# A cross-attention and quantized feed-forward block: in the last batch the first 512 queries of three head groups run ahead of all second halves, and the softmax division is done in parts of 8 heads

## The chip, the core and the metric

One core of one Trainium2 chip runs the kernel. The time is the device time of one execution in microseconds, the median of three runs before the change: 1045.96 (1043.35 to 1048.77).

The engines named below run side by side, each through its own list of instructions in order: PE (TensorE, matrix products; PEld is its loading of weights), DVE (VectorE), ACT (ScalarE), POOL (GpSimd) and SP (here only a queue that issues DMAs). An instruction that waits holds up everything behind it on its engine.

## What is computed

```python
# x: (4, 1024, 256); mem: (4, 77, 256); 16 heads of 16
def xattn(x, mem, Wq, Wkv, Wout, bout):
    q = x @ Wq
    k, v = split(concat((mem, x), axis=1) @ Wkv, 2)      # 77 + 1024 keys
    dots = einsum('bhid,bhjd->bhij', q, k) * 16 ** -0.5
    dots = where(j > i + 77, -inf, dots)                 # a query sees mem and what is not after it
    out = einsum('bhij,bhjd->bhid', softmax(dots), v)
    return merge_heads(out) @ Wout + bout

def ffn(x, w_fc, b_fc, w_proj, b_proj):                  # hidden 1024
    h = gelu(lowprec_linear(x, w_fc, b_fc))              # inputs and weights rounded to 3 mantissa
    return lowprec_linear(h, w_proj, b_proj)             # bits, one exponent per 32 elements

x = x + xattn(layernorm(x), mem, ...)
x = x + ffn(layernorm(x), ...)
```

## The kernel before

**Groups.** The 16 heads of a batch are four groups of four, so there are 16 groups `kk` in all, `last` = 15; the last batch is groups 12 to 15. Four heads lie on four 32-row strips of the partitions, so that four matmuls with 32 rows can run in the array side by side. The 1024 queries are two halves `ic` of 512, the 1101 keys nine tiles of 128.

**Two passes.** The scores of a group are computed twice. The first pass (`max_matmul`, L518, with `max_reduce`, L542 and L544 on DVE) gives the largest score of each query, negated by way of the keys: row `MXR` of each 32-row strip of `qT` takes the maximum, and the same row of `kT` holds -1, so that the second pass (`score_matmul`, L582) comes out with the maximum taken away. ACT then takes the exponential (`score_exp`, L593), POOL masks the tiles on the diagonal (L598), and `times_v` (L619) multiplies by the values. A column of ones beside the values gives the sum of each query's row.

**Order.** `score_pieces` lists 14 pieces of keys by queries: five for the first 512 queries (widths 512, 461, 333, 205, 77), nine for the second (five of 512, then 461, 333, 205, 77). `max_pieces` has 14 pieces of the same widths. `run(kk, extras)` walks over the 14 pieces, each in two half-steps of two heads: in `half_step` the maxima of group `kk + 1` and the scores of group `kk` alternate on PE. The product with the values follows one piece later (`LAG`, the list `late`). Group 15 has no maxima beside it (`last_step`). After piece 1 and after the first half's maxima `put_max` turns 32x32 blocks on DVE (L552), writes them to DRAM and reads them back into row `MXR` of `qT`, two DMAs on SP, long before they are needed.

**Other work among the half-steps.** Each call of `run` takes a list of units; after every half-step it begins units whose turn has come and whose `ready` holds, and `tick` emits the later stages of those begun. The units are: loading and norm of the next batch, projections to q, k and v, and for the batch before: `divide_unit` (softmax division), `wout_unit` (output projection and residual, L716 to L724), `root_unit` (inverse standard deviation by three Newton steps, on POOL while attention runs, L162 to L168), `in_unit` (norm L220/L224, rounding L183 to L206, turn L775), `hidden_unit` (first linear layer L794 and L799, Gelu L805) and `out_unit` (rounding L183 to L206, turn L846, second layer L854 and L857, residual L861, store). A unit covers 128 tokens, a tile; a batch has eight. `helper[0]` is POOL during attention and DVE at the end; POOL does the second rounding step (L206) always.

**Division.** `pack` copies a finished group (L641), places it in `o_pk` by DMA, and writes its row sums to DRAM (L646). When all four groups of a half are packed, `divide_unit(b, ic)` reads the 16 rows of sums spread over 128 partitions (L664), inverts them (L670), writes them (L672), reads each of the 16 rows back over 16 partitions (L678, 16 issues on SP), and multiplies `o_pk` in two products of 128x512 (L687). `rb` has one buffer.

**The last batch.** Groups 12 to 15 carry the units of batch 2. With group 15 come the output projections of the first half of batch 3, if it is divided in time. After the last product a list (`todo`) holds the rest: division of the second half, and for all eight tiles of batch 3 projection, norm, hidden layer and output, DVE being the helper.

**PSUM.** `ps_st` (two buffers of two banks) holds scores and hidden rows, `ps_s` (three banks) maxima and everything small, `ps_av` (one bank) the product with the values.

Of the kernel before, what the change touches and what calls it, by code (L numbers as in the profile page):

```python
# [13 lines left out]
ALU = mybir.AluOpType  # L14
# [29 lines left out]
def kernel(  # L44
# [185 lines left out]
    with ExitStack() as actx:  # L230
# [6 lines left out]
        rbp = ap("rbp", 1)  # L237
# [324 lines left out]


# [67 lines left out]
        divided = set()  # L631
# [26 lines left out]
        def divide_unit(b, ic):  # L658
            got = {}

            def fetch():
                held["rb"] += 1
                got["sm"] = small.tile([P, ICW // SPH], F32, name="sm", bufs=2)
                nc.sync.dma_start(  # L664
                    out=got["sm"], in_=sums.pop((b, ic)).rearrange("h (s j) -> (h s) j", s=SPH)
                )

            def invert():
                r = small.tile([P, ICW // SPH], F32, name="r", bufs=2)
                nc.vector.reciprocal(r, got["sm"])  # L670
                got["rd"] = dram.tile([HEADS, ICW], F32, name="rd")
                nc.sync.dma_start(out=got["rd"].rearrange("h (s j) -> (h s) j", s=SPH), in_=r)  # L672
                got["rb"] = rbp.tile([P, KC, ICW], F32, name="rb")
# [10 lines left out]
            def scale_sums(k):  # L684
                def emit():
                    o = o_pk[b, ic][:, k, :]
                    helper[0].tensor_tensor(o, o, got["rb"][:, k, :], ALU.mult)  # L687
                    if k == KC - 1:
                        divided.add((b, ic))
                        held["rb"] -= 1  # L690
                return emit

            fetch.ready = lambda: packed.get((b, ic)) == NG and not held["rb"]
            stages = [fetch, (4, invert)]
            stages += [(LATER if h == 0 else 1, spread(h)) for h in range(0, HEADS, 2)]
            return cost(0.6, stages + [(4, scale_sums(0)), (2, scale_sums(1))])
# [7 lines left out]
        def wout_unit(b, it):  # L704
# [25 lines left out]
            fetch.ready = lambda: (b, ic) in divided and len(x2) - done["out"] < X2  # L730
# [241 lines left out]
        def run(kk, extras):  # L972
# [8 lines left out]
            rate = sum(price(u) for u in extras) / (2 * sum(length[:-1]))  # L981
            share = 0.0
            for n in range(STEPS):
                for pair in range(2):
# [12 lines left out]
                    if n == 1 and pair == 0 and kk >= 0:  # L997
                        put_max(kk, 1)
                    if n == HALF_AT + 2 and pair == 0 and kk + 1 < B * NG:
                        put_max(kk + 1, 0)  # L1000
# [31 lines left out]
        for kk in range(last + 1):  # L1032
# [15 lines left out]
            if g == NG - 1:  # L1048
                urgent += [divide_unit(b, 0), divide_unit(b, 1)]
# [24 lines left out]
            if kk == last:  # L1074
                helper[0] = nc.vector
                extras += wout_units(b, 0) + [root_unit(b, 0)]
            run(kk, extras)
        while late:
# [48 lines left out]
```

## Time and profile before

| | us |
|---|---|
| median of three runs | 1045.96 |
| the profiled execution | 1048.25 |
| its span | 1046.5 |
| PE busy | 981.6 |
| DVE busy | 652.6 |
| ACT busy | 564.9 |
| POOL busy | 360.0 |
| group 13 with the maxima of 14 | 803.7 to 866.2 |
| group 14 with the maxima of 15 | 866.2 to 921.8 |
| group 15 alone, to its last product | 921.8 to 964.2 |
| after the last product | 964.2 to 1046.5 |
| largest idle gaps of PE between 30 and 960 | 2.54 (at 801.0), 2.41 (562.5), 2.40 (319.4), 1.01 (384.3) |

A row of PE is busy from its start to a modelled end, and a wait for a buffer hidden in it does not show; the distance between equal instructions does. "PEclk" is the clock that TensorE was granted, 1.00 being full: at 0.50 every matmul takes about twice as long. A row of the timeline gives start, duration, engine, line, operation, tiles and shapes, and in brackets the engine's idle time before it with what ended it. A row of the busy times by stage gives the stretch, its length, for each engine the busy time with the number of instructions, then the clock, the share of the DMA engines and GB/s.

### The profile page before, as it was taken

What the parts mean: (1) busy time and instruction counts of PE and PEld (TensorE: products, weight loads), DVE (VectorE), ACT (ScalarE), POOL (GpSimd) and SP (SyncE); (2) the same over time, 40 slices, a digit from 0 to 9 for tenths busy, and PEclk for the clock granted to TensorE, in tenths of its full rate; (3) what the DMA queues carried; (4) which work ended last, traced back from release to release, by engine and by line L of the source; (5) the groups of instructions that cost most, each with busy time, mean ns of one, the idle gap of its engine ahead of it and who ended that gap; (6) DMA issues with size and microseconds to landing.
All of it is one profiled execution on the core that took longest, in us unless ns stands there. A gap on an engine that the chain in (4) does not pass through costs nothing.

```text
span 1046.5 us, 21087 instructions
## 1 busy us (share of the span) xinstructions
PE 981.6 (94%) x8024; PEld 416.2 (40%) x8024; DVE 652.6 (62%) x2127; ACT 564.9 (54%) x838; POOL 360.0 (34%) x751
## 2 busy tenths in 40 slices
PE   4899999999999999999998999999998999999677
PEld 2343434343433344344444344334443334334233
DVE  3587775666484756566475665746557476652785
ACT  4235664555464655655454665665554565666233
POOL 1012422132234444342434253424335246242233
PEclk9899999999998999999998999999997899989576
DMA  3021000202120001101220001100121000001200
GB/s 105 22 67 50 13 26 8 70 13 80 47 73 8 7 10 46 28 7 38 82 70 23 8 15 34 36 11 20 27 69 41 23 8 23 12 13 50 63 21 21
DMA packets 36172, 36.31 MB, mean 35 GB/s; under 512 B 14067, under 2 KB 29747, under 8 KB 36070
## 3 DMA queue, kind: packets, MB, share of 16 engines
q1 hardware_dynamic: 34958, 33.90, 11.8%
q8 instruction: 63, 1.03, 0.4%
q10 hardware_dynamic: 1112, 1.06, 0.3%
q14 instruction: 39, 0.32, 0.1%
HBM read 16.58 MB, written 5.25 MB: 21 GB/s over the span
## 4 chain that ended last, share of the span: by engine, by line
PE 79%; DVE 9%; ACT 3%; DMA 2%; POOL 2%; issue 2%; SPq 1%; POOLq 0%; ACTq 0%; DVEq 0%
PE s_ps L518 35%; PE av_ps L619 16%; PE s_ps L441 6%; PE st_ps L582 5%; PE s_ps L412 3%; PE st_ps L794 3%; PE s_ps L716 3%; DVE jk L544 3%; PE s_ps L854 2%; PE st_ps L799 2%; ACT pt L593 2%; DVE mx L542 1%; PE s_ps L846 1%; DVE amaxh L183 1%; PE s_ps L373 1%
## 5 line engine op out<-in xcount | busy, mean ns | idle before, releaser
L518 PE MATMUL s_ps<-kT,qT 32*128 32x512 f32 (+2 forms) x1736 | 491.8, 537 | 15.0 <-DVE mxp L544 8.2
L593 ACT ACTIVATE pt<-st_ps 128x1024 f32<-128x1024 f32 (+4 forms) x448 | 353.1, 793 | 271.6 <-PE st_ps L582 245.0
L582 PE MATMUL st_ps<-qT,kT 32*128 32x512 f32 (+5 forms) x1792 | 482.4, 534 | 7.4 <-ACT pt L593 6.9
L518 PEld LDWEIGHTS s_ps<-kT,qT 32*128 32x128 f32 x1736 | 194.5, 187 | 189.8 <-issue 70.5
L598 POOL TENSOR_SCALAR_AFFINE_SELECT pt<-pt 128x254 f32<-128x254 f32 (+3 forms) x320 | 117.4, 370 | 431.9 <-ACT pt L593 428.3
L544 DVE CUSTOM_DVE_ANT_0 jk<-s_ps,tri,mx 128x77 bf16<-128x77 f32 (+3 forms) x372 | 174.2, 505 | 97.9 <-PE st_ps L582 63.6
L619 PE MATMUL av_ps<-pt,vaug 128*32 128x256 f32 (+7 forms) x3072 | 223.8, 365 | 2.4 <-POOL hq L206 1.2
L544 DVE CUSTOM_DVE_ANT_0 jk<-s_ps,tri 128x512 bf16<-128x512 f32 (+3 forms) x248 | 126.7, 549 | 142.8 <-PE st_ps L582 103.0
L542 DVE TENSOR_REDUCE mx<-s_ps 128x1 f32<-128x512 f32 x248 | 159.4, 683 | 85.6 <-PE st_ps L582 70.3
L582 PEld LDWEIGHTS st_ps<-qT,kT 32*128 32x128 f32 (+1 forms) x1792 | 186.5, 184 | 21.2 <-ACT pt L593 17.8
L619 PEld LDWEIGHTS av_ps<-pt,vaug 128*32 128x32 f32 (+1 forms) x3072 | 62.3, 109 | 194.7 <-issue 136.6
L206 POOL TENSOR_TENSOR hq<-h,magh 128x512 bf16<-128x512 f32 x64 | 68.4, 1072 | 34.6 <-DVE h L205 27.7
L205 POOL TENSOR_TENSOR h<-h,magh 128x512 f32<-128x512 f32 x40 | 42.0, 1049 | 51.6 <-DVE magh L194 51.1
L701 ACT COPY y<-s_ps 128x256 f32<-128x256 f32 x64 | 23.9, 374 | 49.7 <-PE s_ps L720 24.4
L805 ACT ACTIVATE h<-st_ps 128x1024 f32<-128x1024 f32 x32 | 32.8, 1024 | 30.0 <-PE st_ps L799 29.9
L794 PE MATMUL st_ps<-wfcT,xqT 128*128 128x512 bf16 x128 | 45.0, 439 | 1.8 <-ACT xqT L778 1.8
L183 DVE TENSOR_REDUCE amaxh<-h 128x16 f32<-128x512 f32 x64 | 42.7, 675 | 5.4 <-ACT h L805 5.4
L716 PE MATMUL s_ps<-wo_sb,o_pk 128*128 128x256 f32 x128 | 42.5, 459 | 1.6 <-DVE o_pk L687 1.6
L544 DVE DVE_READ_ACCUMULATOR2_ANT mxp<- 128x1 f32 x512 | 42.0, 82 | 0.0
L412 PE MATMUL s_ps<-wv,xT 128*128 128x256 f32 (+1 forms) x144 | 40.9, 410 | 1.0 <-DVE mx L542 1.0
L441 PE MATMUL s_ps<-xT,wk_sb 128*128 128x512 f32 (+1 forms) x96 | 39.0, 534 | 0.0
L854 PE MATMUL s_ps<-wprT,hT 128*128 128x256 bf16 x256 | 36.4, 289 | 2.6 <-ACT hT L849 2.6
(105 smaller groups left out, 795.2 us busy)
## 6 DMA issues: line engine op xcount, KB each, us to landing
kT<-k_st SPq DMA_DIRECT2D x16, 275.2 KB
xn<-in_x_dram SPq DMA_DIRECT2D x16, 256.0 KB
qT<-q_st SPq DMA_DIRECT2D x16, 256.0 KB
o_pk<-o_st SPq DMA_DIRECT2D x32, 128.0 KB
rb<-rd SPq DMA_DIRECT2D x128, 32.0 KB
x<-in_x_dram SPq DMA_DIRECT2D x32, 128.0 KB
out_dram<-x SPq DMA_DIRECT2D x32, 128.0 KB
x<-in_L_ffn_w_fc_dram SPq DMA_DIRECT2D x8, 128.0 KB
```

Of the source, the lines that this page charges most:

```text
L206: nc.gpsimd.tensor_tensor(dst.rearrange("p (n k) -> p n k", k=QBLK), src3, magb, ALU.subtract)
L412: nc.tensor.matmul(vp[:nj, :], xT[b][:, k, jt * P : jt * P + nj], wv[:, k, :], start=(k == 0), stop=(k == KC - 1),)
L441: nc.tensor.matmul(pp[:, :n], w[:, k, hi * P : (hi + 1) * P], xT[b][:, k, first + lo : first + lo + n], start=(k == 0), stop=(k == KC - 1),)
L518: nc.tensor.matmul(sp[:, 0 : hi - lo], qTs[kk % NQK][rows, it * P : (it + 1) * P], kTs[kk % NQK][rows, lo:hi], start=True, stop=True,)
L542: nc.vector.tensor_reduce(into, sp[:, 0:w], axis=AX.X, op=ALU.max)
L544: nc.vector.tensor_tensor_reduce(junk.tile([P, ICW], BF16, name="jk")[:, 0:w], sp[:, 0:w], mask, 1.0, before, ALU.add, ALU.max, into)
L582: nc.tensor.matmul(st[:nj, e, : i1 - i0], kTs[kk % NQK][rows, t * P : t * P + nj], qTs[kk % NQK][rows, i0:i1], start=True, stop=True,)
L593: nc.scalar.activation(pt[:nj, :, :w], st[:nj, :, :w], AF.Exp, scale=scale)
L598: nc.gpsimd.affine_select(out=pt[:nj, :, :behind], in_=pt[:nj, :, :behind], compare_op=ALU.is_ge, fill=0.0, base=base, pattern=[[0, 2], [1 ...
L619: nc.tensor.matmul(acc[c * PAD : (c + 1) * PAD, off + lo : off + hi], vaugs[b % 2][:nj, t, v0 : v0 + PAD], pts[kk, n, c // 2][:nj, c % 2, ...
L716: nc.tensor.matmul(yp, o_pk[b, ic][:, k, it * P % ICW : it * P % ICW + P], wo_sb[:, k, :], start=(k == 0), stop=False,)
L794: nc.tensor.matmul(hp[:, n, :], xqT[t][:, k, :], wfcT[:, k, n * ICW : (n + 1) * ICW], start=(k == 0), stop=False,)
```

## The change

Three things. First, `divide_unit(b, ic, k)` now divides the 8 heads of part `k`; for all batches it is queued after groups 1 and 3, with four `rb` issues per stage, and `rb` has two buffers of half the size. Second, the groups 13, 14 and 15 run in the order: first halves of 13, 14, 15, then second halves of 13, 14, 15; the maxima of the next group run beside them as before, by halves. Third, where a half's maxima are needed by the stage that follows at once (groups 14 and 15, each half), `next_max` first finishes the products that are outstanding and `add_max` then copies the maxima into a cleared tile (128x512, in the space of the other batch's values), lets TensorE transpose it in four 128x128 blocks into a PSUM tile, and adds this to the half of `qT` on DVE; the DMAs of `put_max` are left out there. Among the second halves stand the units of the first half of batch 3 (projection, norm, hidden layer, output); the list after the last product holds those of the second half alone.

```diff
-        rbp = ap("rbp", 1)
+        rbp = ap("rbp", 2)
...
+        def add_max(kk, half):
+            NI = ICW // P
+            wide = vaugs[(B - 2) % 2].rearrange("p j n -> p (j n)")[:, 0:ICW]
+            nc.vector.tensor_copy(
+                wide.rearrange("p (i c r) -> p c i r", i=NI, r=PAD)[:, :, :, MXR],
+                mxps[kk % 2][:, half * HPG * NI : (half + 1) * HPG * NI].rearrange(
+                    "p (c i) -> p c i", i=NI
+                ),
+            )
+            tp = s_tile([P, ICW])
+            for i in range(NI):
+                nc.tensor.transpose(
+                    tp[:, i * P : (i + 1) * P], wide[:, i * P : (i + 1) * P], ident
+                )
+            q = qTs[kk % NQK][:, half * ICW : (half + 1) * ICW]
+            nc.vector.tensor_tensor(q, q, tp, ALU.add)
+
+        def clear_wide():
+            nc.gpsimd.memset(vaugs[(B - 2) % 2].rearrange("p j n -> p (j n)")[:, 0:ICW], 0.0)
...
-        def divide_unit(b, ic):
+        def divide_unit(b, ic, k):
             got = {}
+            SPK = P // HPC
             def fetch():
                 held["rb"] += 1
-                got["sm"] = small.tile([P, ICW // SPH], F32, name="sm", bufs=2)
+                got["sm"] = small.tile([P, ICW // SPK], F32, name="sm", bufs=2)
...
             def spread(h):
                 def emit():
-                    for i in range(h, h + 2):
+                    for i in range(h, h + 4):
                         nc.sync.dma_start(
-                            out=got["rb"][i % HPC * HD : (i % HPC + 1) * HD, i // HPC, :],
+                            out=got["rb"][i * HD : (i + 1) * HD, :],
                             in_=got["rd"][i, :].partition_broadcast(HD),
                         )
                 return emit
...
+            def scale_sums():
+                o = o_pk[b, ic][:, k, :]
+                helper[0].tensor_tensor(o, o, got["rb"], ALU.mult)
+                divided[b, ic] = k + 1
+                held["rb"] -= 1
+            fetch.ready = lambda: packed.get((b, ic), 0) >= (k + 1) * HPC // HPG and held["rb"] < 2
+            return cost(0.6, [fetch, (4, invert), (2, spread(0)), (1, spread(4)), (3, scale_sums)])
...
-        for kk in range(last + 1):
+        for kk in range(last - 2):
...
-            if g == NG - 1:
-                urgent += [divide_unit(b, 0), divide_unit(b, 1)]
+            if g % 2:
+                urgent += [divide_unit(b, ic, g // 2) for ic in range(NIC)]
...
+            if g == 0 and b == B - 1:
+                extras.append(clear_wide)
             run(kk, extras)
+        b, f = B - 1, B - 2
+        urgent += [divide_unit(b, ic, k) for k, ic in ((0, 0), (1, 0), (0, 1), (1, 1))]
+        early, late_steps = range(HALF_AT + 1), range(HALF_AT + 1, STEPS)
+        def next_max(kk, half, unit=None):
+            if unit is not None and unit[0].ready():
+                begin(unit.pop())
+            while late:
+                k2, n2 = late.popleft()
+                times_v(k2, n2, 0)
+                times_v(k2, n2, 1)
+            tick()
+            add_max(kk, half)
+        outs = [out_unit(t) for t in T]
+        ins = [in_unit(t) for t in T]
+        burst = [hidden_unit(T[:HN])]
+        run(last - 2, [root_unit(f, 1)], early)
+        next_max(last - 1, 0, burst)
+        run(last - 1, burst + outs[:2] + ins[HN : HN + 2], early, False)
+        next_max(last, 0)
+        run(last, ins[HN + 2 :] + outs[2:3], early, False)
+        out2 = outs[3:HN] + [hidden_unit(T[HN:])] + outs[HN : HN + 1]
+        run(last - 2, out2 + wout_units(b, 0), late_steps, False)
+        next_max(last - 1, 1)
+        T = range(b * NT, b * NT + HN)
+        ins = [in_unit(t) for t in T]
+        run(last - 1, outs[HN + 1 :] + [root_unit(b, 0)] + ins, late_steps, False)
+        next_max(last, 1)
+        helper[0] = nc.vector
+        run(last, [hidden_unit(T)] + [out_unit(t) for t in T], late_steps, False)
...
-        T = range((B - 1) * NT, B * NT)
-        todo = urgent + carry
-        chain = lambda ts: [f for t in ts for f in (in_unit(t), hidden_unit([t]), out_unit(t))]
-        todo += merge(chain(T[:HN]), wout_units(B - 1, 1)) + [root_unit(B - 1, 1)]
-        todo += chain(T[HN:])
+        T = range(b * NT + HN, (b + 1) * NT)
+        todo = urgent + wout_units(b, 1) + [root_unit(b, 1)] + carry
+        todo += [f for t in T for f in (in_unit(t), hidden_unit([t]), out_unit(t))]
```

`run` takes the range of pieces as `steps`, and leaves `put_max` out with `puts=False`.

More of the change, by code (lines that the diff above doesn't have):

```diff
@@ L630 @@
         packed = {}
-        divided = set()
+        divided = {}
         def pack(b, ic, g, acc):
@@ L656 @@
         SPH = P // HEADS
-        def divide_unit(b, ic):
+        def divide_unit(b, ic, k):
             got = {}
+            SPK = P // HPC
             def fetch():
                 held["rb"] += 1
-                got["sm"] = small.tile([P, ICW // SPH], F32, name="sm", bufs=2)
+                got["sm"] = small.tile([P, ICW // SPK], F32, name="sm", bufs=2)
                 nc.sync.dma_start(
-                    out=got["sm"], in_=sums.pop((b, ic)).rearrange("h (s j) -> (h s) j", s=SPH)
+                    out=got["sm"],
+                    in_=sums[b, ic][k * HPC : (k + 1) * HPC, :].rearrange("h (s j) -> (h s) j", s=SPK),
                 )
             def invert():
-                r = small.tile([P, ICW // SPH], F32, name="r", bufs=2)
+                r = small.tile([P, ICW // SPK], F32, name="r", bufs=2)
                 nc.vector.reciprocal(r, got["sm"])
-                got["rd"] = dram.tile([HEADS, ICW], F32, name="rd")
-                nc.sync.dma_start(out=got["rd"].rearrange("h (s j) -> (h s) j", s=SPH), in_=r)
-                got["rb"] = rbp.tile([P, KC, ICW], F32, name="rb")
+                got["rd"] = dram.tile([HPC, ICW], F32, name="rd")
+                nc.sync.dma_start(out=got["rd"].rearrange("h (s j) -> (h s) j", s=SPK), in_=r)
+                got["rb"] = rbp.tile([P, ICW], F32, name="rb")
             def spread(h):
                 def emit():
-                    for i in range(h, h + 2):
+                    for i in range(h, h + 4):
                         nc.sync.dma_start(
-                            out=got["rb"][i % HPC * HD : (i % HPC + 1) * HD, i // HPC, :],
+                            out=got["rb"][i * HD : (i + 1) * HD, :],
                             in_=got["rd"][i, :].partition_broadcast(HD),
@@ L682, in spread @@
                 return emit
[L684 to L696, printed above, removed]
+            def scale_sums():
[5 more added lines that the diff above has]
+            return cost(0.6, [fetch, (4, invert), (2, spread(0)), (1, spread(4)), (3, scale_sums)])
         def evacuate(ps):
@@ L728, in collect @@
                 done["wout"] += 1
-            fetch.ready = lambda: (b, ic) in divided and len(x2) - done["out"] < X2
+            fetch.ready = lambda: divided.get((b, ic)) == KC and len(x2) - done["out"] < X2
             return cost(1.8, [fetch, project, (2, add), (2, collect)])
@@ L970, in last_step, with run @@
                 score_exp(kk, n, pair, sts[pair])
-        def run(kk, extras):
+        def run(kk, extras, steps=None, puts=True):
             extras = carry + list(extras)
@@ L980, in run @@
             length = [150 + p[3] - p[2] for p in PIECES]
-            rate = sum(price(u) for u in extras) / (2 * sum(length[:-1]))
+            steps = steps or range(STEPS)
+            rate = sum(price(u) for u in extras) / (2 * sum(length[n] for n in steps[:-1]))
             share = 0.0
-            for n in range(STEPS):
+            for n in steps:
                 for pair in range(2):
@@ L996, in run @@
                             late.popleft()
-                    if n == 1 and pair == 0 and kk >= 0:
+                    if puts and n == 1 and pair == 0 and kk >= 0:
                         put_max(kk, 1)
-                    if n == HALF_AT + 2 and pair == 0 and kk + 1 < B * NG:
+                    if puts and n == HALF_AT + 2 and pair == 0 and kk + 1 < B * NG:
                         put_max(kk + 1, 0)
@@ L1073 @@
                     extras += side[:1] + qs + merge(vs, side[1:])
-            if kk == last:
-                helper[0] = nc.vector
-                extras += wout_units(b, 0) + [root_unit(b, 0)]
+            if g == 0 and b == B - 1:
+                extras.append(clear_wide)
             run(kk, extras)
+        b, f = B - 1, B - 2
[27 more added lines that the diff above has]
+        run(last, [hidden_unit(T)] + [out_unit(t) for t in T], late_steps, False)
         while late:
```

## The prediction

> **What bounds the kernel now.** I read the page first (span, and the row of the granted clock), then the busy time by stage from group 13 to the end, TensorE's idle gaps in its timeline, and the end of the chain of waits.
>
> ```profile
> span 1046.5 us, 21087 instructions
> ...
> PEclk9899999999998999999998999999997899989576
> ```
>
> The clock of TensorE is full but for short dips a batch apart and the last three slices. "Early" below means the five pieces of a group for the first 512 queries, "late" the nine for the second.
>
> ```profile
> core 0: us, PE busy (x) PEld busy (x) DVE busy (x) ACT busy (x) POOL busy (x), PEclk, DMA share, GB/s
> 803.70:866.16 62.46, 61.88 (x498) 24.96 (x494) 37.40 (x124) 34.64 (x47) 23.98 (x46) 0.89 0.05 13
> 866.16:921.78 55.62, 54.59 (x495) 21.86 (x491) 35.73 (x117) 35.47 (x50) 24.67 (x50) 1.00 0.05 17
> ...
> 964.17:1012.23 48.06, 33.66 (x140) 15.41 (x140) 36.62 (x107) 15.77 (x26) 11.86 (x12) 0.72 0.16 47
> 1012.23:1046.50 34.27, 24.43 (x100) 9.33 (x100) 21.81 (x50) 10.65 (x16) 11.45 (x12) 0.60 0.06 20
> ```
>
> Groups 13 and 14 are TensorE's. Group 15 takes 42.4 us, 921.8 to 964.2. What follows its last product, 82.3 us, is a chain of latencies: TensorE is idle 24 us of it and has a clock of 0.72 and 0.60 in the rest. The change works on these 82 us, and on a gap a batch apart, of which this is the last:
>
> ```profile
> 796.53 1.28 POOL L687 TENSOR_TENSOR o_pk<-o_pk,rb 128x512 f32<-128x512 f32 x1
> ...
> 799.44 1.09 ACT L224 ACTIVATE xh<-x,shift,rstd 128x256 f32<-128x256 f32 x2 [3.37 <-POOL shift L168]
> ...
> 800.98 0.41 PE L582 MATMUL st_ps<-qT,kT 32*77 32x77 f32 x1 [2.54 <-ACT pt L593]
> ```
>
> GpSimd's division product (L687) delays the last Newton step of the norm; ScalarE, already at the norm, waits; its exponentials wait behind, then TensorE. The clock pays more than the gap:
>
> ```profile
> 800.00:805.00 5.00, 4.02 (x36) 2.42 (x38) 4.69 (x19) 2.79 (x8) 3.45 (x6) 0.56 0.00 0
> ...
> 815.00:820.00 5.00, 5.00 (x39) 2.13 (x37) 2.22 (x9) 2.52 (x4) 0.82 (x2) 0.74 0.18 56
> ...
> 930.00:935.00 5.00, 5.00 (x60) 2.21 (x55) 0.97 (x2) 2.84 (x5) 4.21 (x7) 0.63 0.04 15
> ```
>
> Half clock from about 800.6 to 817.6 costs 8.5 us. The gaps at 317.0 and 560.1 (2.40 and 2.41 us, TensorE behind VectorE) bring half clock for 10.2 us each, 5.1 us lost. Two gaps of 0.69 and 0.82 us within 4 us, at 924 and 927, bring 6.8 us of it (3.4 lost). A lone gap of 0.70 (939.7) brings none. So between 0.7 and about 1.1 us of idleness in some 3.4 us, the clock halves for 6.8 us or more.
>
> **The change part by part.** Changes count against this execution's span; the execution took 1048.25 us in all, 2.3 above the median of 1045.96, and I put the sum on the median.
>
> *The end, after the last product.*
>
> ```profile
> 965.91 1.69 DMA sums<-o_st
> 967.61 1.80 DMA sm<-sums
> 969.44 0.56 DVE r L670
> 970.02 1.59 DMA rd<-r
> ```
>
> From 964.2 to the first issue of `rb` at 971.6 nothing changes (7.4; the reciprocal is half as wide, no credit). Sixteen issues took 7.55 us on SP; eight remain, 3.8. They land 1.8 later (the row above), the product is 0.7 on VectorE: 13.8. Then four projections at half clock, 2.0 + 0.34 each as at 989.5, less one half that now stands before the wait: 8.3. Evacuation, add and statistics of the last 1.4, inverse root 3.4 (1008.9 to 1012.3), and the second half's chain, unchanged in order, 34.3. On SP two stores of the first half's results now stand ahead of `rd`; their adds end 2.1 after the last product (1.2 + 0.4 + 0.4), `rd` is due at 5.9. Sum 61.2 against 82.3: **-21.1**. Below it can go by some 3 us if the projections find full clock (1.27 each).
>
> *The first half's work moves in among the attention.* Per tile at full clock: projection 1.27, turn 0.21, hidden layer 1.63 (910.35 to 916.87 is four), turn of the hidden row 0.55, output 1.19: 4.85. Four tiles 19.4; one output (1.2) stays behind the last product: **+18.2**. This is the point that decides: TensorE pays for nearly all that the end saves. Not all: where maxima run, a half-step is longer than its matmuls.
>
> ```profile
> 891.31 0.64 PE L619 MATMUL av_ps<-pt,vaug 128*32 128x256 f32 x8
> 891.88 1.05 PE L854 MATMUL s_ps<-wprT,hT 128*128 128x256 bf16 x8
> 893.93 0.64 PE L619 MATMUL av_ps<-pt,vaug 128*32 128x256 f32 x8
> 895.82 0.64 PE L619 MATMUL av_ps<-pt,vaug 128*32 128x256 f32 x8
> ```
>
> A bare half-step takes 1.89 (893.93 to 895.82); one with an output of 1.19 takes 2.62, so 0.73 is paid and about 0.4 is hidden behind the wait for VectorE's maxima. In the order of the changed program some nine pieces (three projections, and three turns and three outputs of batch 2 that stood in group 15) come to lie there: **-3.6** (0 to -8).
>
> *Maxima by TensorE.* Four `put_max` go: four 0.2 us VectorE transposes and eight DMAs on SP, both with room, nothing gained. In their place, four times: a VectorE copy 128x16 (0.2 by the 128x32 transpose at L552), four transposes (sixteen at L373 took 3.68: 0.92), a VectorE add 128x512 (0.69 to 1.11 by L687's rows on VectorE). Transposes: **+3.7** (up to 5.2 by L373's mean of 324 ns). The wait: every score of the next stage is queued on TensorE behind the add. Ahead of group 14 one max matmul lies between (and the hidden burst or projections cover copy and drain): 0.5 each, twice. Ahead of group 15's early half nothing does: 0.85, and 0.35 for the output that waits for its copy. Ahead of its late half the products wait for a mask that stands on GpSimd behind two 0.62 us roundings: 1.2 + 0.9. Together **+4.3** (1.5 to 9).
>
> *Ramps.* Each half drains its products and starts without any under the maxima, and in group 15 the hidden burst takes two table loads (1.28) and four Gelus (1.02) from a ScalarE that paces it: **+1.8** (0 to 5).
>
> *Clock.* Group 15's early half has its dip already. Ahead of the late half 2.1 us idle is over the bound, so one more dip of 6.8 us: **+3.5** (0 to 14, if all four stages dip).
>
> The page "TensorE: Matmul & The Clock Gate" (section "Why this matters for your kernels") warns only of idle gaps over about 3 us; by it this term is nothing and the sum 3.5 lower, but the rows here dip after 2.4 us and after 0.69 + 0.82, and they decide. The same page (Part 4) says that transposes do not count as busy in the same way, which speaks against this change: by it each transition idles 0.9 us more, all four dip, and the sum is 10 higher; no row here shows it.
>
> *Division in parts.* Per batch four units for two; 128 issues of `rb` as before, eight more `sm`, `rd` and reciprocals, on SP and VectorE off the path. What matters is where the GpSimd product stands. In the new order none stands in the norm at the start of a batch. At 801 the norm starts 1.2 earlier, the gap shrinks to 1.3, and I take three windows of half clock for five: **-4.6** (-1.2 to -11). At 317 and 560 a VectorE magnitude took 1.04 us under L687 and 0.38 is left under the rounding that follows (0.61): 0.55 each, gap 1.85, clock as before: **-1.1** (0 to -15). The products' new places meet VectorE elsewhere; they cost nothing while VectorE is 60% busy, as at the start of each batch now.
>
> Sum: -21.1 + 18.2 - 3.6 + 3.7 + 4.3 + 1.8 + 3.5 - 4.6 - 1.1 = +1.1, so **1047 us**.
>
> **The rivals.** *The clock falls at each new transition* (slower). Place: before early 14, early 15, late 14, late 15. Price: 3.4 to 5.1 each, three more than I counted, 10 to 15: about 1060. It decides once idleness passes 1.1 us in 3.4; the transposes' neighbours are light products, and 924 to 927 shows that such work dips. Against it: a dense burst or projections stand before two of the four.
>
> *The batch stalls close* (faster). If the shortened gaps fall under the bound at 801 (another -6.4) and one of 317 and 560 (-6.9 with its rest): 1034. For it: 1.3 us is near the bound. Against: the four tiles' magnitudes still stand in one row on VectorE.
>
> *Group 15 swallows the moved work* (faster). Its 42.4 us hold only about 31 us of matmuls (scores 11.7 and products 12.1 by rows of their widths at full clock, 7.0 of batch 2); the rest waits for exponentials and at half clock. If the hidden layers and outputs fill that, -8: 1039. Against: they bring 8 us to ScalarE too.
>
> *The move does not happen*: excluded, since in the new order only one output of the first half follows the last product.
>
> **How the numbers follow.** The forecast (1040 to 1054 its own range) 0.48; clock at the transitions 0.25; batch stalls 0.14; group 15 0.13. A measurement can tell 0.5%, 5.2 us, from no change. Of the forecast 0.34 lies within that, 0.11 above, 0.03 below; of the slower rival 0.01 within; so faster 0.30, same 0.35, slower 0.35. The range 1034 to 1060 reaches to the other cases.
>
> **What would show it.** After the last product some 61 us, with eight `rb` issues; the last product of group 15 some 21 us later than 964 less what the batch stalls give; idle gaps of 0.5 to 2 us before the four stages and the clock row beside each; at 317 and 560 gaps near 1.9, at 800 near 1.3 with a shorter dip. I am wrong if the half clock after the last product lasts less, if the half-steps of 13 and 14 hide more or less than 0.4 us a piece, or if a transition idles over 3 us.

## The result, and the profile after

The changed kernel takes 1076.24 us (median of 4 runs, 1072.08 to 1077.12), against 1047.05 for the kernel before in the same comparison (1043.35 to 1048.77): a ratio of 1.0263, 95% interval 1.0232 to 1.0293. It is slower by 29 us. The prediction was 1047 us, no change, with a range up to 1060: wrong. The profiled execution has a span of 1075.0 us for 1046.5, 28.5 longer, and these are placed below.

The page of the changed kernel, its span and its row of granted clocks (40 slices):

```profile
span 1075.0 us, 21156 instructions
...
PEclk9889999999998989999999999999997889995956
```

The dip a batch apart is still there at 810 (the seven after the long row of nines), now with the two eights of the reordered groups behind it, and there is a new hole, the 5 that is fourth from the end: group 15's late half. By stages, one line each: early halves of groups 13, 14, 15, late halves of 13, 14, 15, what follows the last product (window, its length, busy time of TensorE, weight loads, VectorE, ScalarE, GpSimd, then the granted clock, DMA share, GB/s):

```profile
810.39:842.88 32.49, 32.34 (x223) 13.27 (x219) 13.50 (x58) 16.01 (x25) 11.78 (x25) 0.79 0.05 15
842.88:867.57 24.69, 21.27 (x174) 9.51 (x174) 16.77 (x61) 12.12 (x18) 17.96 (x37) 0.79 0.07 18
867.57:884.04 16.47, 13.20 (x113) 5.38 (x113) 3.69 (x10) 9.00 (x17) 10.82 (x19) 0.79 0.08 26
884.04:927.82 43.78, 43.18 (x381) 18.45 (x377) 25.40 (x67) 27.48 (x35) 17.84 (x27) 1.00 0.11 32
927.82:970.66 42.84, 36.90 (x335) 16.89 (x334) 32.77 (x93) 22.45 (x32) 27.30 (x49) 0.96 0.08 20
970.66:1016.88 46.22, 42.63 (x287) 15.43 (x287) 14.85 (x27) 25.80 (x33) 13.60 (x18) 0.70 0.03 10
1016.88:1075.00 58.12, 32.11 (x129) 13.86 (x129) 29.25 (x79) 14.72 (x24) 11.44 (x12) 0.63 0.10 30
```

Length times one less the clock is what a stage lost to the throttle, if TensorE paces it. With that the two executions compare like this (us; the stages of before are 803.70 to 964.17 and what follows):

| part | before | after | difference |
|---|---|---|---|
| to the start of group 13 | 803.7 | 810.4 | +6.7 |
| groups 13 to 15, without the clock's loss | 150.2 | 175.4 | +25.2 |
| groups 13 to 15, lost to the clock | 10.3 | 31.1 | +20.8 |
| after the last product | 82.3 | 58.1 | -24.2 |
| span | 1046.5 | 1075.0 | +28.5 |

The second and fourth rows are the trade that the change makes, and they nearly cancel, as forecast (+24.4 and -21.1 there). The loss is in the other two. The largest piece is one place, the transition from group 14's late half to group 15's. TensorE's timeline there (start, length, engine, line, operation, tiles, count, and in brackets the idle time before it and what ended it):

```profile
963.73 0.84 PE L642 MATMUL av_ps<-pt,vaug 128*32 128x167 f32 x16
968.00 0.49 PE L642 MATMUL av_ps<-pt,vaug 77*32 77x77 f32 x8 [3.44 <-POOL pt L621]
...
968.82 1.06 PE L577 MATMUL s_ps<-ident,vaug 128*128 128x128 f32 x4
970.66 2.09 PE L605 MATMUL st_ps<-qT,kT 32*128 32x512 f32 x8 [0.78 <-DVE qT L581]
...
973.94 1.01 PE L815 MATMUL st_ps<-wfcT,xqT 128*128 128x512 bf16 x2 [0.65 <-ACT pt L616]
...
985.78 3.40 PE L605 MATMUL st_ps<-qT,kT 32*128 32x512 f32 x8
991.93 3.00 PE L605 MATMUL st_ps<-qT,kT 32*128 32x512 f32 x8 [2.75 <-ACT pt L616]
```

(An fp32 matmul shows as two records, so x8 are four matmuls.) The last product waits 3.44 us for a mask (L621) on GpSimd. GpSimd was not idle; its own timeline shows what stood ahead of the two masks:

```profile
962.84 0.73 POOL L882 TENSOR_TENSOR x<-x,y 128x256 f32<-128x256 f32 x1
963.52 0.62 POOL L205 TENSOR_TENSOR xh<-xh,magx 128x256 f32<-128x256 f32 x1
964.22 0.62 POOL L206 TENSOR_TENSOR xq<-xh,magx 128x256 bf16<-128x256 f32 x1
964.79 0.62 POOL L205 TENSOR_TENSOR xh<-xh,magx 128x256 f32<-128x256 f32 x1
965.49 0.63 POOL L206 TENSOR_TENSOR xq<-xh,magx 128x256 bf16<-128x256 f32 x1
966.08 0.32 POOL L621 TENSOR_SCALAR_AFFINE_SELECT pt<-pt 77x152 f32<-77x152 f32 x1
966.38 0.61 POOL L205 TENSOR_TENSOR xh<-xh,magx 128x256 f32<-128x256 f32 x1
967.06 0.62 POOL L206 TENSOR_TENSOR xq<-xh,magx 128x256 bf16<-128x256 f32 x1
967.63 0.32 POOL L621 TENSOR_SCALAR_AFFINE_SELECT pt<-pt 77x152 f32<-77x152 f32 x1
```

An add and six roundings of the first half's input units. And the clock, in windows of 1 us (the granted clock is the third number from the end):

```profile
967.00:968.00 1.00, 0.00 (x0) 0.00 (x0) 0.00 (x0) 0.00 (x0) 0.94 (x3) 0.65 0.00 0
...
997.00:998.00 1.00, 1.00 (x5) 0.52 (x8) 0.00 (x0) 0.00 (x0) 0.00 (x0) 0.50 0.00 0
998.00:999.00 1.00, 1.00 (x15) 0.29 (x12) 0.00 (x0) 0.27 (x1) 0.00 (x0) 0.99 0.00 0
```

It falls about 2.7 us into the idle time and comes back 30 us later, some 15 us of work lost: the hidden layer of four tiles (L815, L820) takes 11.8 us, to the next scores, for 6.5 at full clock, and a second wait of 2.75 us for ScalarE follows it.

### The profile page after: what moved, and what is told of

It reads as the page before. It is cut to its first block, busy times and chain, and to the rows that moved or that the text cites. A ratio compares the mean times of both kernels' runs of the same rounds, so it can differ in the third digit from the quotient of the medians.

```text
span 1075.0 us, 21156 instructions
## 1 busy us (share of the span) xinstructions
PE 994.9 (93%) x8040; PEld 421.0 (39%) x8040; DVE 639.5 (59%) x2098; ACT 569.7 (53%) x844; POOL 382.5 (36%) x789
## 3 DMA queue, kind: packets, MB, share of 16 engines
q10 hardware_dynamic: 1112, 1.06, 0.3%
## 4 chain that ended last, share of the span: by engine, by line
PE 74%; POOL 7%; DVE 7%; ACT 4%; issue 3%; DMA 3%; SPq 1%; POOLq 0%; ACTq 0%; DVEq 0%
PE s_ps L518 31%; PE av_ps L642 14%; PE s_ps L441 6%; PE st_ps L605 5%; PE s_ps L737 3%; PE s_ps L412 3%; PE st_ps L815 3%; PE s_ps L875 2%; ACT pt L616 2%; DVE mx L542 2%; PE st_ps L820 2%; DVE jk L544 2%; POOL pt L621 2%; POOL h L205 1%; POOL hq L206 1%
## 5 line engine op out<-in xcount | busy, mean ns | idle before, releaser
L518 PE MATMUL s_ps<-kT,qT 32*128 32x512 f32 (+2 forms) x1736 | 497.1, 540 | 15.0 <-DVE mxp L544 6.9
L605 PE MATMUL st_ps<-qT,kT 32*128 32x512 f32 (+5 forms) x1792 | 489.1, 545 | 10.4 <-ACT pt L616 8.5
L621 POOL TENSOR_SCALAR_AFFINE_SELECT pt<-pt 128x254 f32<-128x254 f32 (+3 forms) x320 | 117.9, 372 | 439.3 <-ACT pt L616 436.6
L544 DVE CUSTOM_DVE_ANT_0 jk<-s_ps,tri,mx 128x77 bf16<-128x77 f32 (+4 forms) x372 | 173.7, 505 | 88.9 <-PE st_ps L605 63.7
L605 PEld LDWEIGHTS st_ps<-qT,kT 32*128 32x128 f32 (+1 forms) x1792 | 188.7, 186 | 26.9 <-ACT pt L616 18.9
L642 PEld LDWEIGHTS av_ps<-pt,vaug 128*32 128x32 f32 (+1 forms) x3072 | 62.5, 109 | 195.8 <-issue 138.0
L205 POOL TENSOR_TENSOR h<-h,magh 128x512 f32<-128x512 f32 x48 | 50.3, 1048 | 56.9 <-DVE magh L194 45.3
L815 PE MATMUL st_ps<-wfcT,xqT 128*128 128x512 bf16 x128 | 45.5, 443 | 2.6 <-ACT xqT L799 1.3
L441 PE MATMUL s_ps<-xT,wk_sb 128*128 128x512 f32 (+1 forms) x96 | 39.2, 536 | 0.0
L870 ACT COPY hT<-s_ps 128x1024 bf16<-128x1024 bf16 x32 | 32.3, 1013 | 11.8 <-PE s_ps L867 11.2
```

The costliest lines, as they stand in the source:

```text
L441: nc.tensor.matmul(pp[:, :n], w[:, k, hi * P : (hi + 1) * P], xT[b][:, k, first + lo : first + lo + n], start=(k == 0), stop=(k == KC - 1),)
L518: nc.tensor.matmul(sp[:, 0 : hi - lo], qTs[kk % NQK][rows, it * P : (it + 1) * P], kTs[kk % NQK][rows, lo:hi], start=True, stop=True,)
L544: nc.vector.tensor_tensor_reduce(junk.tile([P, ICW], BF16, name="jk")[:, 0:w], sp[:, 0:w], mask, 1.0, before, ALU.add, ALU.max, into)
L605: nc.tensor.matmul(st[:nj, e, : i1 - i0], kTs[kk % NQK][rows, t * P : t * P + nj], qTs[kk % NQK][rows, i0:i1], start=True, stop=True,)
L621: nc.gpsimd.affine_select(out=pt[:nj, :, :behind], in_=pt[:nj, :, :behind], compare_op=ALU.is_ge, fill=0.0, base=base, pattern=[[0, 2], [1 ...
L642: nc.tensor.matmul(acc[c * PAD : (c + 1) * PAD, off + lo : off + hi], vaugs[b % 2][:nj, t, v0 : v0 + PAD], pts[kk, n, c // 2][:nj, c % 2, ...
```

## The experiments

Ratios are against the kernel before, on the same chip, with 95% intervals. Theories: the clock at the transitions (A); the masks behind GpSimd's roundings, which bring it about (B); the division in parts, through SP's queue (C); and the rival to all three, that the reordered work itself costs more than the end saves (D).

### Each part of the change alone

`parts_only` is the kernel before with the new `divide_unit`, two `rb` buffers and this:

```
-            if g == NG - 1:
-                urgent += [divide_unit(b, 0), divide_unit(b, 1)]
+            if g % 2:
+                urgent += [divide_unit(b, ic, g // 2) for ic in range(NIC)]
```

> The kernel before with the division in parts alone, the order of the last batch untouched. If the parts cost what the trace of after shows up to the start of group 13 (6.7 us later, with new dips of the clock at 387 and 632 us), less the 3.8 us that eight issues of rb fewer save after the last product, it is about 3 us slower than before (0.3%), with the start of group 13 near 810. If those 6.7 us were a chance of that one execution, the batch stalls give what I forecast, 5.7, and the end 3.8: some 9 us faster.

1056.41 us, 1.0107 (1.0053 to 1.0161): slower by about 9, more than C asked. Group 13 starts at 808.9 (803.7 before). Group 0, ahead of any division, ends between 113.2 and 120.3 us in the profiled executions, so it has to be taken out: from its end to the start of group 13 the two executions with the old division take 687.8 us (before) and 686.6 (`order_only`, below), the six with the parts and nothing else changed up to there 692.5 to 695.4. So the parts cost some 5 to 9 us ahead of group 13. The batch stall at 801 does shrink: its gap is 1.28 for 2.54, and group 13 loses 1.2 us to the clock for 6.9. But what follows the last product takes 88.3 us for 82.3, with a clock of 0.60 for 0.67.

`order_only` is the changed kernel with the old, whole division:

```
-        urgent += [divide_unit(b, ic, k) for k, ic in ((0, 0), (1, 0), (0, 1), (1, 1))]
+        urgent += [divide_unit(b, 0), divide_unit(b, 1)]
```

> The changed kernel with the division of before (whole, one rb buffer), the new order of the last batch kept. If the loss lies in the last batch, group 13 starts near 804 as before, the last batch is as slow as in after and the end some 4 us longer for its sixteen issues of rb: 1071 to 1075, still 2.5% slower than before. If the loss came from the parts, it comes down to within 1% of before.

1064.50 us, 1.0178 (1.0131 to 1.0226), so 17 us slower: the two parts of the change add up to nearly its whole loss, and both lose. Its groups 13 to 15 take 192.6 us for 160.5 (10 of the 32 are the clock's) and its end 65.2 for 82.3. The loss is less than expected, and the trace says why. Its late half of group 15:

```profile
959.50:997.00 37.50, 34.02 (x283) 13.39 (x285) 15.91 (x42) 25.80 (x34) 14.64 (x33) 0.95 0.05 16
```

37.5 us at 0.95 for 46.2 at 0.70. The input units wait for the projections, these for the division, and the whole division ends later: so the roundings fell behind the transition by themselves, and TensorE idles 0.78 us there, not 3.44. The loss at that place takes both parts of the change together.

### The transition ahead of group 15's late half

`filled` gives TensorE something to do in the 3.44 us and leaves the wait as it is:

```
+            for _ in range(5):
+                nc.tensor.matmul(sp, ident, kTs[0][:, 0:ICW], start=True, stop=True)
             while late:
```

> The changed kernel with five idle-filling fp32 matmuls 128x512 (about 0.75 us each at full clock) on TensorE ahead of the last four products of group 14's late half, where it now idles 3.44 us; the wait itself stays. If the clock is the cost (it falls at the end of that idle time and stays at half for 30 us), it stays at full now, the late half of group 15 takes about 35 us for 47.5, and the time falls by some 11 to 13 us to about 1064. If the wait and the light work of the last group are the cost, whatever stands before, the time is within 3 us of after.

1070.60 us, 1.0222 (1.0183 to 1.0262): 5.6 us less than the changed kernel, half of what A said. Its TensorE:

```profile
962.61 4.56 PE L1108 MATMUL s_ps<-kT,ident 128*128 128x512 f32 x10
967.10 0.69 PE L642 MATMUL av_ps<-pt,vaug 128*32 128x205 f32 x16
...
969.34 1.14 PE L605 MATMUL st_ps<-qT,kT 32*128 32x512 f32 x8 [0.78 <-DVE qT L581]
...
983.93 3.00 PE L605 MATMUL st_ps<-qT,kT 32*128 32x512 f32 x8 [2.75 <-ACT pt L616]
```

The spare work covers the wait (L1108; five matmuls, 0.9 us each), the next scores take 1.14 us for 2.09 and the clock is full up to 982: idle time was what brought it down. The second wait of 2.75 us, for ScalarE behind the Gelus, now brings a dip of its own. The stage takes 39.2 us; it lost 10.4 us less to the clock and became 7.1 shorter; presumably some of ScalarE's work had been hidden behind the slow TensorE.

`late_ins` takes the cause of the wait away:

```
-        run(last - 1, outs[HN + 1 :] + [root_unit(b, 0)] + ins, late_steps, False)
+        run(last - 1, outs[HN + 1 :] + [root_unit(b, 0)], late_steps, False, 4.8)
...
-        run(last, [hidden_unit(T)] + [out_unit(t) for t in T], late_steps, False)
+        run(last, ins + [hidden_unit(T)] + [out_unit(t) for t in T], late_steps, False)
```

(4.8 keeps the pace of the units that stay.)

> The changed kernel with the four input units of the first half of batch 3 moved from the end of group 14's late half to the start of group 15's, so that no rounding stands ahead of the last masks on GpSimd. If the masks' place behind the roundings makes the 3.44 us, the idle time there falls to 1.0 to 1.5 us; if the clock then stays up, the late half of group 15 comes to 34 to 37 us and the time to about 1062; if the clock dips but the dense fp32 work that now follows brings it back in 7 us, about 1065. If the half clock belongs to the work of group 15's late half, the time falls by 2 to 3 us only.

1066.09 us, 1.0178 (1.0124 to 1.0232), 10 under the changed kernel. Its TensorE at the same place:

```profile
962.61 1.30 PE L642 MATMUL av_ps<-pt,vaug 128*32 128x167 f32 x24
964.30 0.66 PE L577 MATMUL s_ps<-ident,vaug 128*128 128x128 f32 x4 [0.39 <-DVE vaug L569]
965.74 1.14 PE L605 MATMUL st_ps<-qT,kT 32*128 32x512 f32 x8 [0.78 <-DVE qT L581]
968.07 2.05 PE L605 MATMUL st_ps<-qT,kT 32*128 32x512 f32 x8 [1.19 <-ACT pt L616]
971.29 3.00 PE L605 MATMUL st_ps<-qT,kT 32*128 32x512 f32 x8 [1.18 <-ACT pt L616]
```

No product waits for a mask: B holds for the wait. The late half of 14 is 5.0 us shorter, that of 15 7.7. Two waits of 1.2 us for exponentials still make the clock dip (the scores at 971 take 3.00 us), and it is back some 6 us after the work resumed.

`burst_test` asks why the clock stayed down for 30 us in the changed kernel and for 6 here. It adds ten spare fp32 matmuls 128x256 (the identity by a weight) to the changed kernel, in `hidden_unit`:

```
+                if tiles[0] == (B - 1) * NT:
+                    warm(10)
```

> The changed kernel with ten spare fp32 matmuls 128x256 ahead of the hidden layer (bf16) of group 15's late half, where the clock is at half and stays there for 18 us of dense work. If it is this kind of work that doesn't bring the clock back, as fp32 does in 6 to 7 us, the ten (9 us at half clock) bring it to full ahead of or early in the hidden layer, which then takes 6.5 to 8 us for 11.9; the time stays within 5 us of after. If the clock stays down for some other reason for 30 us, the ten only add some 9 us to the time and the hidden layer takes 11.9 again.

1074.43 us (2 runs), 1.0246 (1.0188 to 1.0304). The wait for the mask is the same 3.43 us, and the clock is at half from 966.1. Then, on TensorE:

```profile
972.88 6.23 PE L962 MATMUL s_ps<-wo_sb,ident 128*128 128x256 f32 x20
978.95 0.38 PE L817 MATMUL st_ps<-wfcT,xqT 128*128 128x512 bf16 x1
...
985.69 1.02 PE L605 MATMUL st_ps<-qT,kT 32*128 32x512 f32 x2
```

and the clock, in windows of 2 us:

```profile
974.00:976.00 2.00, 2.00 (x7) 1.55 (x6) 0.00 (x0) 1.98 (x4) 0.00 (x0) 0.50 0.00 0
976.00:978.00 2.00, 2.00 (x10) 1.77 (x9) 0.00 (x0) 0.44 (x1) 0.00 (x0) 0.92 0.00 0
```

The spare fp32 work (first window) has the clock back at about 976.3, 3.4 us after it began (and 5.9 after the scores at 970.46, which run into it without a gap), and the hidden layer takes 6.7 us for 11.8. In the changed kernel 11.8 us of the hidden layer, with no gap in it, had not brought it back. The stage loses 6.3 us to the clock for 13.9, and the time stays, since the ten cost what they save.

`dma_turn` puts the old way of bringing the maxima into the four transitions:

```
-            add_max(kk, half)
+            put_max(kk, half)
```

> The changed kernel with its four transitions as before the change: the maxima turned by VectorE and brought to the queries by two DMAs each, not by TensorE. If TensorE's turn is no part of the loss, each transition now idles 3 us or more for the DMAs (landing times of 1.5 to 1.8 us twice) where TensorE's way took 1.4: the time grows by 5 to 12 us, to 1081 to 1088. If the transposes at TensorE themselves cost (work and clock), it falls under 1074.

1095.15 us, 1.0478 (1.0412 to 1.0543), 19 over the changed kernel. The first score of each of the four stages:

```profile
850.30 1.19 PE L605 MATMUL st_ps<-qT,kT 32*128 32x512 f32 x1 [5.14 <-DMA qT<-md]
880.47 2.09 PE L605 MATMUL st_ps<-qT,kT 32*128 32x512 f32 x8 [5.83 <-DMA qT<-md]
944.78 1.19 PE L605 MATMUL st_ps<-qT,kT 32*128 32x512 f32 x1 [3.92 <-DMA qT<-md]
995.26 2.09 PE L605 MATMUL st_ps<-qT,kT 32*128 32x512 f32 x8 [5.99 <-DMA qT<-md]
```

20.9 us of idle time where TensorE's turn has 0.78 twice and nothing twice. In this order TensorE's turn is the cheaper of the two ways by 19 us; its own price, some 3 us of transposes and the 0.78 us twice, lies in the 25.2 above.

### The parts, and the fetch of the context rows

In `parts_only` SP's queue, and then TensorE at the end of group 5, read:

```profile
381.73 0.36 SPq L860 DMA_DIRECT2D out_dram<-x  x1
382.19 0.33 SPq L389 DMA_DIRECT2D xh<-in_ctx_dram  x1
```

```profile
384.19 0.32 PE L394 MATMUL s_ps<-ident,xh 77*128 77x77 f32 x2 [1.51 <-DMA xh<-in_ctx_dram]
```

The fetch (L389) stands behind a store that waits for GpSimd's add, before the change too; the eight `rb` ahead of it were through by 372. But with the batch stall shorter, TensorE now gets there sooner, and a wait of 0.3 to 1.0 us without a dip becomes one of 1.5 to 1.7 with one. The saving of the stall is given back at the next fixed point, and the clock adds to it: group 6 takes 65.0 us for 63.2. `parts_mem` moves the fetch:

```
-            units[1].append(mem_unit(b))
+            units[1].insert(HN + 1, mem_unit(b))
```

> The kernel with the division in parts alone, and the fetch of the context rows (xh from in_ctx) issued ahead of the norm units of its half batch instead of behind them. In the parts the fetch stood on SP behind rd, sixteen rb and a store, and TensorE waited 1.5 to 1.7 us for it at the end of the second group of a batch (0.5 to 1.0 before), after which the clock dipped. If that is what the parts cost, the wait goes, groups 6 and 7, 10 and 11 fall back by 2.1 to 3.5 us each pair to 120.3 as before, and the time comes to about 1051, 5 us under the parts alone. If the extra issues or the place of the products themselves cost it, the wait goes and the time stays near 1056.

1052.36 us, 1.0052 (1.0018 to 1.0086), 4 under `parts_only`. The two intervals overlap, so the lengths of the groups have to show it. SP's queue now has the fetch 20 us ahead of the store:

```profile
365.98 0.33 SPq L389 DMA_DIRECT2D xh<-in_ctx_dram  x1
...
386.81 0.36 SPq L860 DMA_DIRECT2D out_dram<-x  x1
```

Groups 6 and 7 take 120.4 us, as before the change (120.3; 123.7 with the parts alone), 10 and 11 the same; groups 4 and 5 take 119.2 for 121.5, 8 and 9 120.4 for 121.8. From the end of group 0 to the start of group 13 it takes 684.9 us, under the 686.6 and 687.8 of the old division and the 692.5 to 695.4 of the parts. Here are the gains that I forecast for the parts, and group 13 adds 4.7 (57.7 for 62.5). C is right, with the place in the queue as its mechanism and not the number of issues. What the parts then still lose lies after the last product: 88.4 us for 82.3.

### Spare work, and versions that could win

`warm_before` is the kernel before, with the same spare matmuls put where TensorE idles: four at each batch boundary, sixteen, two and eight ahead of turns after the last product, two ahead of each output of the last batch:

```
+                    if kk > 0 and kk % NG == 0 and n == STEPS - 1 and pair == 0 and e == 0:
+                        warm(4, tops[0])
...
+                if t in WARM_IN:
+                    warm(WARM_IN[t])
```

> The kernel before, with spare fp32 matmuls 128x256 (0.45 us each) on TensorE where it idles: four at each batch boundary (the gaps of 2.4 to 2.5 us), sixteen, two and eight ahead of three turns after the last product, two ahead of each output of the last batch. They compute nothing that is used. If half clock follows idle time of TensorE and a busy TensorE keeps it away, the dips at 317, 560 and 800 go (some 9 us) and part of the 27 us lost after the last product, on the path by half: 1025 to 1035. If the clock falls for another reason, the spare work only adds: 1047 to 1055.

1043.85 us, 0.9955 (0.9924 to 0.9987). A little faster, far from 1025 to 1035. After the last product the clock is 0.87 for 0.67, and that stretch gets 2.9 us shorter, though it loses 17 less to half clock:

```profile
963.19:1042.60 79.41, 67.69 (x323) 39.04 (x324) 58.77 (x156) 26.51 (x42) 23.28 (x24) 0.87 0.13 37
```

So TensorE's clock does not set the pace of most of that stretch; a chain through GpSimd, ScalarE and VectorE would explain it, but what the spare work itself costs there was not separated. Of the three boundaries the dips at 317 and 560 went, that at 801 stayed (7.0 us lost).

`after_fixed` is the changed kernel with `late_ins`, the early fetch, and spare matmuls at the boundaries, the four transitions and three steps of group 15 (`best_b` adds those after the last product).

```
+            warm(2)
             while late:
                 k2, n2 = late.popleft()
...
             add_max(kk, half)
+            warm(1)
```

> The changed kernel with the input units late (as before in late_ins), the context rows fetched early, and spare fp32 matmuls of 0.45 us: two at each batch boundary, two ahead of the drain and one after the transposes at each of the four transitions, two at three steps of group 15 that wait for exponentials. After it nothing stands behind the roundings. If clock and fetch are what the change loses, 5 us come back in batches 1 and 2, some 7 at 810 and 9 to 10 in groups 13 to 15 beside late_ins: about 1045, as fast as before. If the order loses by its own work, it stays at 1058 or above.

1052.63 us, 1.0062 (1.0032 to 1.0093): 21 (by the ratios) to 24 (by the medians) of the 29 us come back, but it is not as fast as before.

```
+                if t >= WARM_OUT:
+                    warm(2)
                 yp = s_tile([P, D])
```

> after_fixed with spare matmuls after the last product too (two ahead of each output of the last batch, sixteen ahead of the first turn of the second half, where TensorE idles 7.8 us, two ahead of the next two). If half clock (24 us lost of 61) lies on the path there as in before's end, where the same brought 3 of 17 us, 1047 to 1050, no faster than before: then the new order by itself gives nothing even without its stalls. If the new order does win once the clock stays up, 1042 or under.

1054.08 us, 1.0066 (1.0038 to 1.0095). The mean clock is 0.977 now, for 0.934 in the changed kernel, and the new order still does not win.

`best_a` is the order of before: parts in batches 0 to 2, the last batch's division whole, the early fetch, two spare matmuls at each boundary and those after the last product. `best_c` has the parts in the last batch too, and twenty spare matmuls at the wait of 9.65 us that `parts_only` shows ahead of the second half's projections.

```
+            if g % 2 and b < B - 1:
+                urgent += [divide_unit(b, ic, g // 2) for ic in range(NIC)]
+            elif g == NG - 1:
+                urgent += [divide_whole(b, ic) for ic in range(NIC)]
```

> The order of before, with the parts in batches 0 to 2 alone, the last batch's division whole, the context rows fetched early, two spare matmuls at each batch boundary, and spare matmuls after the last product as in warm_before. If the last product falls near 960 (the parts with the early fetch had 961.8 with 2.3 us of later work pulled in) and 79.4 follow as in warm_before: 1039 to 1042, some 0.6% faster than before. If the longer end of the parts alone (88 us for 82) came from batches 0 to 2 and not from the division in the last batch, 1046 to 1050.

```
                 for k in range(KC):
+                    if k and t == (B - 1) * NT + HN:
+                        warm(20)
                     nc.tensor.matmul(
                         yp, o_pk[b, ic][:, k, it * P % ICW : it * P % ICW + P], wo_sb[:, k, :],
```

> The parts with the early fetch in all batches, two spare matmuls at each batch boundary, and after the last product twenty ahead of the second division's projection (idle 9.65 us there), four and eight ahead of two turns, two ahead of each output. If the 88 us that follow the last product with the parts are the clock's (0.60, never back to full), they come down to 78 to 82: 1040 to 1045. If they are the order in which TensorE takes the projections, the end stays near 86 and the time near 1048.

`best_a`: 1038.08 us, 0.9897 (0.9862 to 0.9932), faster than both kernels. `best_c`: 1045.60, 0.9971 (0.9945 to 0.9996); its end takes 88.4 us at a clock of 0.81, as long as at 0.60 in `parts_only`, so it is not the clock that costs there; the order in which TensorE takes the projections may, and was not tried. The row of `best_a` shows no dip but in the first slices and after the last product (one of 3.4 us in group 15 does not show in slices of 26 us):

```profile
span 1039.5 us, 21325 instructions
...
PEclk9799999999999999999999999999999999999889
```

Against `best_a`, `best_b` shows the order with everything mended on both sides (the last batch's division in parts here, whole there): its groups 13 to 15 take 192.9 us for 154.5 (8.8 of the 38.4 are the clock's, 10.6 lost for 1.8; some 5, an estimate from twelve of 0.45, are the spare matmuls at the transitions), and its end 60.2 for 83.9. D is right too: by itself the order buys 24 us with about as much work, the transitions' spare work and clock come on top.

## Why the prediction was wrong, point by point

- *The end, -21.1*: -24.2. Right, and on the low side as allowed, but not by the reason given: the projections did not find full clock. It was at half until 1035.6, so that only the last of the four tiles ran at full, and all four took 7.1 us for 8.3; the second half's chain took 32.5 for 34.3, the rest is small. Eight issues of `rb` (3.6 us), as said.
- *Moved work, hidden part, transposes, waits, ramps*: +18.2 - 3.6 + 3.7 + 4.3 + 1.8 = +24.4; groups 13 to 15 grew by 25.2 without the clock's loss. The sum is right; its terms were not taken apart one by one, and since the wait below alone is 2 us longer than its term, some other term must have erred the other way: the match is partly luck. Within it the transposes took 0.61 to 1.06 us each time, about 3 in all for 3.7.
- *The wait ahead of group 15's late half*, "the products wait for a mask that stands on GpSimd behind two 0.62 us roundings: 1.2 + 0.9". **Here the prediction failed first.** All four input units become ready at one moment, when the inverse root ends, and six roundings and an add stood there: 3.44 + 0.78 us. That is also the prediction's own sign of being wrong, a transition that idles over 3 us. `late_ins` and `order_only`, without them, have no such wait.
- *Clock, +3.5*, "one more dip of 6.8 us". **This is the step that decided**: +20.8, beyond the term's own 0 to 14. The late half of 15 lost 13.9 us and the end of 14's 1.7, not 3.4: half clock lasted 30.7 us. The prediction listed dips of 17.0, 10.2, 10.2 and 6.8 us and priced this one by the shortest. What runs behind the wait has a part in the length: the hidden layer followed, under which the clock stayed down, while with spare work ahead of it the clock came back (`burst_test`); and then came the wait of 2.75 us for ScalarE, which the forecast had only as table loads among the ramps. Early 14 lost 5.2 more, where I counted nothing; early 15 lost 3.5, as before.
- *Division in parts, -4.6 and -1.1*: group 13's start is 6.7 later, 2.0 of it from group 0 (which ends at 117.9 for 115.9), and the dip at 810 came as before (6.8 lost, 6.9 before). The gaps went to 1.19 to 1.30 as forecast or better, and the stalls did close in `parts_mem`. "On SP and VectorE off the path" was the wrong sentence: TensorE arrives sooner at a fetch that comes no sooner.
- *The rivals.* "The clock falls at each new transition" was right in its sign, priced at 10 to 15 us with 3.4 to 5.1 a dip; it came at two of its four places (early 14, late 15). At late 15 its cause is shown (`filled`) and it cost 15.6; at early 14 the idle time was far under the 1.1 us that it asked for. Ahead of late 14 four transposes ran 0.66 us and the clock stayed at full, so the sum of 10 more, with all four transitions dipping, did not come either. "The batch stalls close" came only with the early fetch. "Group 15 swallows the moved work" did not come. The range ended at 1060 because each dip had one price in it.

The page "TensorE: Matmul & The Clock Gate" of the Trainium skill (sections "Part 1: The HAM clock gate" and "Why this matters for your kernels") says that a window of about 3.4 us of sustained activity opens the clock and that an idle window of that order closes it. The run of spare fp32 matmuls agrees with the first (3.4 us). The hidden layer does not: 11.8 us of it opened nothing, nor did 16.6 us of fp32 half-steps in the kernel before (below). Nor do gaps of 1.2 to 1.3 us, which closed it in some executions here.

The record shows two more things about the dips. First, fp32 work does not always bring the clock back. The dip at 801 in the kernel before lies under fp32 maxima, scores and products, with a few transposes between them and an output projection from 815.7 on, and by its rows TensorE was busy throughout:

```profile
801.00:817.60 16.60, 16.46 (x90) 6.98 (x90) 9.68 (x34) 7.36 (x14) 8.74 (x17) 0.50 0.03 7
```

Second, in all fourteen profiled executions half clock lasts a whole multiple of 3.41 us (but where the execution ends) (6.8, 10.2 and 17.1 in the kernel before, 30.7 in the changed one, 68.3 after the last product of `parts_only`), and within an execution all changes of the clock lie on one grid of that step. So 3.4 us in `burst_test` and about 6 in `late_ins` do not rank two kinds of work. The grid fits what the gap of 1.28 to 1.30 us at the last batch boundary did: it brought half clock in six executions (3.4 us in `parts_only` and `filled`, 6.8 in `burst_test`, 13.7 in the changed kernel, `late_ins` and `dma_turn`), where all or nearly all of it lay between two grid points, and none in `parts_mem`, where a grid point cut it into 0.76 and 0.52. This is read from the traces; no run tried it.

What stays open: half clock begins in early 14 at 847.8 with no wait there over 0.67 us (`after_fixed` has it too, with one of 0.58), under the 0.7 us that the prediction took as harmless; which property of the work brings the clock back (the hidden layer is bf16, with a three-row bias matmul that takes a third of its time, but the half-steps are fp32); and why the end takes 83.9 us in `best_a` and 79.4 in `warm_before`, with nearly the same spare work. None was tried by itself.

## What to carry to other kernels

When work is moved into a stage, list for each in-order queue what will stand ahead of the one instruction that the next stage waits for; units that become ready at the same moment arrive together, so the wait is their sum. Price a wait on TensorE by what follows it, not by its own length: 3.4 us cost 15 here because the work behind it did not bring the clock back, and the cure was to move four units by one stage. And a stall that is shortened hands its time to the next fixed point, here a DMA behind a store: move that too before judging the change.

## What the hardware showed that was not expected

- At half clock, 11.8 us of hidden layer without a gap (bf16 128x512 and bias matmuls of three rows) left the clock at half, and so did 16.6 us of fp32 maxima, scores and products in the kernel before. Ten spare fp32 matmuls 128x256 brought it back in 3.4 us, and the last group's fp32 scores and products, with no maxima beside them, in about 6.
- Matmuls that compute nothing that is used, put into TensorE's idle time, keep the clock at full (966 to 982 in `filled`), and after the last product a mean clock of 0.87 for 0.67 went with only 2.9 us of 82.
- Half clock lasted whole multiples of 3.41 us in every execution, and the same gap of 1.3 us at one place was followed by 0, 3.4, 6.8 or 13.7 us of it; near that length a price has to be two-sided.
